# Moving 195 of 8832 row gathers from GpSimd to SyncE, row by row

## The chip, the cores and the metric

The kernel runs on one core of a Trainium2 chip. The metric is device time in microseconds, from the start of the program to its end. Five engines work beside each other, each with its own queue of instructions: TensorE (PE), VectorE (DVE), ScalarE (ACT), GpSimd (POOL) and SyncE (SP). Transfers between the chip's memory and the on-chip buffers are issued by SyncE or GpSimd and carried out by 16 DMA engines that both share.

## The reference

A recommendation model scores 16384 users. Each has 69 ids of a table of 100001 embeddings of 96 numbers, and one label id. For every (user, id) pair the embedding `u` and the label's embedding `q` go through a small attention network, which gives one weight; the weighted embeddings are summed in 10 groups and go through three dense layers.

```
u   = emb[batch_user]                          # (16384, 69, 96)
ql  = emb[batch_label[:, 0]];  q = broadcast(ql)
z   = concat([q, u, q - u, q * u])             # (..., 384)
h   = dice(z @ W1 + b1, a1)                    # 64
att = (h @ W2 + b2) @ W3 + b3                  # one number
pre = where(batch_user < ITEM_NUM, u * att, 0)
pooled = einsum('gf,bfe->bge', window, pre)    # 10 groups
x   = concat([pooled, ql])
x   = dice(bn(x @ Wf1 + bf1));  x = dice(bn(x @ Wf2 + bf2))
out = x @ Wf3 + bf3
```

`dice(x)` is `(alpha (1 - p) + p) x` with `p` the sigmoid of `x` scaled. What matters here is the first line: 16384 x 69 rows of 384 bytes, scattered over the table, must be fetched.

## The kernel before

The users are cut into 32 blocks of 512 (`NBLK`, `BLK`). A block has 69 chunks (`NCH`) of 512 (user, id) pairs: 64 main chunks, in each of which 8 users stand with 64 ids (`NMAIN`), and 5 tail chunks, each with one further id for all 512 users (`NTAIL`). Two chunks make a pair of chunks, the step of the main loop; there are 32 x 69 / 2 = 1104 pairs (`NPAIR`). "Pair" means this below.

A chunk's rows come as four tiles of 128 rows, one row per partition. Each tile is one indirect DMA, issued by GpSimd in `gather`:

```python
gather(rows, u[:, 4 * j + t, :], ids[n][:, 4 * k + t : 4 * k + t + 1])
nc.tensor.transpose(ptr[:, t * P : (t + 1) * P], u[:, 4 * j + t, :], ident)
```

So a pair has 8 gathers, into a buffer `u` of a pool of 14 (`upool`), and the kernel has 1104 x 8 = 8832. Each block has 4 more gathers for its labels (`head_gather`), 128 in all. In `fetch`, TensorE transposes each of the four tiles into one PSUM buffer `ptr`; VectorE multiplies that with the label's embedding (`quT`) and ScalarE copies it (`uT`). `hidden` makes the first layer of the attention network two pairs later, `attend_rows` and `spread` the weights, and `pool(i)`, 7 pairs later (`POOL_LAG`), multiplies the same rows `u` with these weights: it is the last reader of a tile of rows. The dense layers of a finished block (`top1`, `top2`, `top3`) are spread over later pairs.

The order of all this is written out by hand: `at(step, work)` puts each piece of work into a plan by pair number, and the plan is run in order under a manual schedule. Each engine's queue keeps that order; only the waits between engines are put in by the framework.

SyncE has 13 DMAs: the first block's ids, two packs of weights (`wn`, `wf`), 8 loads of ids for 4 blocks each (`load_ids`, planned 20 pairs ahead of their first use), and two stores of the result.

Of the kernel before, what the change touches and what calls it, by code (L numbers as in the profile page):

```python
# [1 line left out]

# [7 lines left out]

F32 = mybir.dt.float32
I32 = mybir.dt.int32
AF = mybir.ActivationFunctionType
ALU = mybir.AluOpType
PSUM = bass.MemoryType.PSUM

P = 128
B, F, E, G = 16384, 69, 96, 10  # L40
ITEM_NUM = 100000
# [5 lines left out]
NBLK = B // BLK  # L47
FM = 64
NTAIL = F - FM
NS = BLK // FM  # L50
NMAIN = BLK // NS
NCH = NMAIN + NTAIL
# [12 lines left out]
EARLY = 20  # L65

CLOSE = 8


class Pack:  # L70
# [44 lines left out]
def rec_kernel(  # L115
# [3 lines left out]
    idx: bass.AP,  # L119
    emb: bass.AP,  # L120
    rows: bass.AP,
    near: bass.AP,
    far: bass.AP,
    out: bass.AP,
):
    nc = tc.nc

    const = ctx.enter_context(tc.tile_pool(name="const", bufs=1))
    ipool = ctx.enter_context(tc.tile_pool(name="ipool", bufs=2))
# [7 lines left out]
    def by_field(ap):  # L137

        return ap.rearrange("e (s o) -> e s o", o=1).to_broadcast([ap.shape[0], NS, FM])

    ids = {0: const.tile([P, NCOL], I32, name="ids0")}
    nc.sync.dma_start(out=ids[0], in_=idx0)

    def load_ids(n):

        t = ipool.tile([P, NIDS, NCOL], I32, tag="ids", name=f"ids{n}")
        nc.sync.dma_start(out=t.rearrange("p b n -> p (b n)"), in_=idx[(n - 1) // NIDS])
        for k in range(NIDS):
            ids[n + k] = t[:, k, :]


    wn = const.tile([P, NEAR.width], F32, name="wn")
    nc.sync.dma_start(out=wn, in_=near)
# [3 lines left out]
    ident = const.tile([P, P], F32, name="ident")  # L157
# [26 lines left out]
    for i in range(2):  # L184
        t = const.tile([E + 1, BLK], F32, name=f"qT{i}")
# [70 lines left out]
    def gather(table, dst, index):  # L256
        nc.gpsimd.indirect_dma_start(  # L257
            out=dst,
            out_offset=None,
            in_=table,  # L260
            in_offset=bass.IndirectOffsetOnAxis(ap=index, axis=0),
        )

    def chunk(c):

        n, k = divmod(c, NCH)
        if n == NBLK - 1 and k >= EARLY:
            k = NMAIN + k - EARLY if k < EARLY + NTAIL else k - NTAIL
        return n, k

    def head_gather(n):

# [28 lines left out]
    def fetch(i, between=None):  # L301

        u = upool.tile([P, 8, E], F32, tag="u", name=f"u{i}")
        uT = []
        quT = tpool.tile([E, 2, 512], F32, tag="quT", name=f"quT{i}")
        for j in range(2):
            if j == 1 and between:
                between()
            n, k = chunk(2 * i + j)
            ptr = ps_tr.tile([E, 512], F32, tag="tr", name=f"ptr{i}_{j}")  # L310
            for t in range(4):
                gather(rows, u[:, 4 * j + t, :], ids[n][:, 4 * k + t : 4 * k + t + 1])
                nc.tensor.transpose(ptr[:, t * P : (t + 1) * P], u[:, 4 * j + t, :], ident)  # L313
            q = qTs[n % 2][0:E]
            if k < NMAIN:
                nc.vector.tensor_tensor(  # L316
                    quT[:, j, :].rearrange("e (s f) -> e s f", f=FM),
                    ptr.rearrange("e (s f) -> e s f", f=FM),
                    by_field(q[:, k * NS : (k + 1) * NS]),
                    ALU.mult,  # L320
                )
            else:
                nc.vector.tensor_tensor(quT[:, j, :], ptr, q[:, 0:BLK], ALU.mult)
            uT.append(room(k))
            nc.scalar.copy(uT[j][0:E], ptr)  # L325
        return u, uT, quT

    def hidden(i, uT, quT):

        ph = ps_h.tile([P, 512], F32, tag="h", name=f"ph{i}")  # L330
        places = [chunk(2 * i + j) for j in range(2)]
# [25 lines left out]

    def attend_tail(i, j, y, uT):

        n, k = chunk(2 * i + j)  # L360
# [26 lines left out]
    def pool(i):  # L387

        u, rw = us.pop(i), rws.pop(i)
        todo = [(j, *chunk(2 * i + j)) for j in range(2)]  # L390
        todo = [(j, n, k) for j, n, k in todo if k < NMAIN]
        if not todo:
            return
        pa = ps_acc.tile([E, 2, NS, G], F32, tag="acc", name=f"acc{i}")
        for j, n, k in todo:
            for t in range(4):
                nc.tensor.matmul(  # L397
                    pa[:, j, 2 * t : 2 * t + 2, :].rearrange("e n g -> e (n g)"),
                    u[:, 4 * j + t, :],
                    rw[:, t, j, :],  # L400
                    start=True,
                    stop=True,
                )
        if len(todo) == 2:
# [98 lines left out]
    def hidden_of(k):  # L503
        return lambda: ys.__setitem__(k, hidden(k, *hs[k]))

    def tails_of(k):
        def work():
            uT = hs.pop(k)[0]
            for j in range(2):
                if chunk(2 * k + j)[1] >= NMAIN:  # L510
                    attend_tail(k, j, ys[k], uT)

        return work

    def fetch_of(k, between=()):
        def work():
            for j in range(2):
                n = chunk(2 * k + j)[0]
# [11 lines left out]
    def at(step, *work):  # L530
        plan.setdefault(step, []).extend(work)

    c = NPAIR - CLOSE
    for i in range(c):
# [6 lines left out]
        if i >= 2:  # L541
            at(i, hidden_of(i - 2))
        if i < c - CLOSE:
            if i >= POOL_LAG:
# [16 lines left out]
    for n in range(NBLK):  # L561
        first, end = n * NCH // 2, ((n + 1) * NCH - 1) // 2
        if n > 0:
            if n % NIDS == 1:
                at(first - 20, lambda n=n: load_ids(n))
            at(first - 14, lambda n=n: qs.__setitem__(n, head_gather(n)))
            at(first - 11, lambda n=n: head_turn(n, qs.pop(n)))
            at(first - 9, lambda n=n: head_rows(n))
        if n < NBLK - 2:
            for s, work in enumerate(top_steps(n, slice(0, BLK))):  # L570
                at(end + POOL_LAG + 4 + s, work)
        elif n == NBLK - 2:
            for s, work in enumerate(top_steps(n, slice(0, BLK))):
                at(end + POOL_LAG + s // 2, work)
    for f in range(NTAIL):
        at(2 + 2 * f, lambda f=f: tail_weights(f))

# [6 lines left out]
    d = NPAIR  # L584
# [75 lines left out]
```

## Time and profile before

| | |
|---|---|
| timed runs | 13386.58, 13436.96, 13456.45 us; median 13436.96 us |
| profiled execution, span of its instructions | 11239.3 us (no other time of that execution is given) |
| GpSimd busy | 8465.4 us, 75% of the span |
| TensorE busy | 9082.8 us, 81% |
| ScalarE, VectorE busy | 3188.3 us, 3014.3 us |
| gathers of rows | 8832, mean 945 ns each |
| bytes read | 446.61 MB, 40 GB/s over the span |
| mean granted TensorE clock | 0.727 |

The profile is that of one execution. All times in it are measured from the span's start. The timed median is 2197.7 us longer than the profiled span. An engine's busy time leaves out instructions that only issue DMAs, set registers or wait, so SyncE has no busy time at all; its DMA issues stand as "SPq" in the timeline. A group's row gives the line, engine, operation, tiles, count and busy time with the mean of one, and behind the bar the idle time in front of these instructions and what ended most of it ("issue": nothing that the profile shows).

### The profile page before, as it was taken

The page shows a single profiled execution, that of the slowest core. Times are in us where ns is not written, and L with a number is a line of the kernel's source. Part 1 is how long each engine was busy: PE and PEld are TensorE (multiplying, and loading weights), DVE is VectorE, ACT ScalarE, POOL GpSimd, SP SyncE. Part 2 cuts the span into 40 slices and gives each one's busy share as a digit, 9 for nine tenths or more (in the row PEclk, how much of TensorE's full clock was granted, in tenths as well). Part 3 has the DMA queues.
Part 4 walks back from the last instruction along what each step waited for, and adds up shares of the span by engine and source line. Part 5 has one row for each costly group of instructions (what it writes and reads, how often), then busy time and mean ns, then how long its engine had stood idle before and what let it go on. Part 6 is the DMA issues. An engine that isn't in the chain of part 4 may idle for free.

```text
span 11239.3 us, 108444 instructions
## 1 busy us (share of the span) xinstructions
PE 9082.8 (81%) x41797; PEld 4395.1 (39%) x41797; DVE 3014.3 (27%) x5325; ACT 3188.3 (28%) x4969; POOL 8465.4 (75%) x8966
## 2 busy tenths in 40 slices
PE   7888888888878787877888778777787887888888
PEld 3333433333433333333333333333343333433335
DVE  3222222222222222222222222222222222222222
ACT  2222222222222222222222222222222222222223
POOL 7777777777777777777777777777777777777776
PEclk6767777677776777777777777777777767777767
DMA  2111111111111111111111111111111111111111
GB/s 49 40 40 40 40 40 42 40 40 40 40 42 40 40 40 40 42 40 40 40 40 42 40 40 40 40 42 40 40 40 40 42 40 40 40 40 40 40 40 35
DMA packets 288946, 454.19 MB, mean 40 GB/s; under 512 B 143538, under 2 KB 143922, under 8 KB 288306
## 3 DMA queue, kind: packets, MB, share of 16 engines
q0 software_dynamic: 286720, 440.98, 18.7%
q8 instruction: 335, 5.49, 0.2%
q1 hardware_dynamic: 1714, 6.28, 0.2%
q14 instruction: 177, 1.45, 0.0%
HBM read 446.61 MB, written 0.07 MB: 40 GB/s over the span
## 4 chain that ended last, share of the span: by engine, by line
POOL 51%; issue 23%; PE 15%; DMA 11%; ACT 0%; DVE 0%; POOLq 0%
POOL u L257 50%; DMA u<-in_rows,ids 11%; PE p L438 4%; PE acc L397 3%; PE ph L342 2%; PE ph L338 2%; PE ptr L313 2%; POOL q L257 1%; PE prow L353 1%; PE ph L335 1%; PE ph L340 0%; PE pc L290 0%; PE pa L362 0%; PE patt L370 0%; PE p L449 0%
## 5 line engine op out<-in xcount | busy, mean ns | idle before, releaser
L257 POOL DMA_INDIRECT u<-in_rows,ids x8832 | 8343.6, 945 | 2690.9 <-issue 2510.2
L313 PE MATMUL ptr<-ident,u 128*96 128x128 f32 x8832 | 2092.4, 336 | 2080.2 <-DMA u<-in_rows,ids 2066.4
L325 ACT COPY uT<-ptr 96x512 f32<-96x512 f32 x2208 | 1285.2, 582 | 4422.4 <-DVE quT L316 4069.1
L313 PEld LDWEIGHTS ptr<-ident,u 128*96 128x96 f32 x8832 | 1184.6, 150 | 2904.1 <-DMA u<-in_rows,ids 2460.6
L397 PEld LDWEIGHTS acc<-rw,u 128*96 128x96 f32 x16384 | 1746.1, 190 | 1206.4 <-issue 1059.7
L346 DVE TENSOR_TENSOR y<-ph,y 128x512 f32<-128x512 f32 x1104 | 763.5, 692 | 4885.1 <-ACT y L345 4703.4
L316 DVE TENSOR_TENSOR quT<-ptr,qT 96x512 f32<-96x512 f32 x2048 | 1375.9, 677 | 2183.2 <-PE ptr L313 2180.0
L397 PE MATMUL acc<-rw,u 128*96 128x20 f32 x16384 | 1852.9, 260 | 23.1 <-DVE rw L375 18.0
L338 PE MATMUL ph<-uT,A 128*64 128x512 f32 x4096 | 1688.2, 902 | 1.0 <-ACT uT L325 1.0
L342 PE MATMUL ph<-quT,wn 96*64 96x512 f32 x4416 | 1628.4, 809 | 0.0
L344 ACT ACTIVATE y<-ph 128x512 f32<-128x512 f32 x1104 | 659.4, 597 | 2971.7 <-PE ph L342 2962.3
L345 ACT ACTIVATE y<-y,wn,na1c 128x512 f32<-128x512 f32 x1104 | 898.1, 814 | 37.3
L342 PEld LDWEIGHTS ph<-quT,wn 96*64 96x64 f32 x4416 | 447.5, 191 | 1070.4 <-issue 1069.8
L438 PE MATMUL p<-pooled,wf 96*100 96x512 f32 (+1 forms) x1400 | 706.2, 654 | 0.0
L338 PEld LDWEIGHTS ph<-uT,A 128*64 128x64 f32 x4096 | 269.0, 179 | 616.0 <-issue 609.8
L406 DVE COPY pooled<-acc 96x160 f32<-96x160 f32 x1008 | 419.9, 417 | 129.4 <-PE acc L397 129.4
L353 PE MATMUL prow<-y,v 128*32 128x512 f32 x2208 | 452.4, 894 | 0.3 <-DVE y L346 0.3
L438 PE MATMUL p<-pre,V 96*100 96x512 f32 (+1 forms) x700 | 398.9, 717 | 2.7 <-DVE x L421 2.3
L438 PEld LDWEIGHTS p<-pooled,wf 96*100 96x100 f32 x1400 | 265.6, 202 | 341.2 <-issue 341.2
L375 DVE SCALAR_TENSOR_TENSOR rw<-patt,bb,wn 128x320 f32<-128x320 f32 x554 | 277.8, 543 | 221.2 <-PE patt L370 220.3
L355 ACT COPY row<-prow 128x512 f32<-128x512 f32 (+1 forms) x277 | 161.8, 584 | 314.5 <-PE prow L353 314.2
L370 PE MATMUL patt<-ident,row 128*128 128x128 f32 x1108 | 231.2, 347 | 15.9 <-DVE pre L363 15.2
(66 smaller groups left out, 2227.6 us busy)
## 6 DMA issues: line engine op xcount, KB each, us to landing
u<-in_rows,ids POOLq DMA_INDIRECT x8832, 2.5
ids<-in_idx SPq DMA_DIRECT2D x8, 560.0 KB, 3.7
q<-in_emb,ids POOLq DMA_INDIRECT x128, 2.5
wf<-in_far SPq DMA_DIRECT2D x1, 1209.0 KB, 7.8
wn<-in_near SPq DMA_DIRECT2D x1, 236.0 KB, 2.7
ids<-in_idx SPq DMA_DIRECT2D x1, 140.0 KB, 2.2
out<-r SPq DMA_DIRECT2D x1, 63.5 KB
out<-r SPq DMA_DIRECT2D x1, 0.5 KB
```

Source lines behind the costliest of these rows:

```text
L257: nc.gpsimd.indirect_dma_start(out=dst, out_offset=None, in_=table, in_offset=bass.IndirectOffsetOnAxis(ap=index, axis=0),)
L313: nc.tensor.transpose(ptr[:, t * P : (t + 1) * P], u[:, 4 * j + t, :], ident)
L316: nc.vector.tensor_tensor(quT[:, j, :].rearrange("e (s f) -> e s f", f=FM), ptr.rearrange("e (s f) -> e s f", f=FM), by_field(q[:, k * NS ...
L325: nc.scalar.copy(uT[j][0:E], ptr)
L338: nc.tensor.matmul(p, As[n % 2][:, k // 4, :], uT[j], start=True, stop=False)
L342: nc.tensor.matmul(p, Wp, quT[:, j, :], start=False, stop=True)
L344: nc.scalar.activation(y, ph, AF.Sigmoid, scale=S_DICE)
L345: nc.scalar.activation(y, y, AF.Identity, bias=a1c, scale=na1c)
L346: nc.vector.tensor_mul(y, ph, y)
L353: nc.tensor.matmul(pr[32 * k : 32 * (k + 1), :], v2, ys[b + k], start=True, stop=True)
L397: nc.tensor.matmul(pa[:, j, 2 * t : 2 * t + 2, :].rearrange("e n g -> e (n g)"), u[:, 4 * j + t, :], rw[:, t, j, :], start=True, stop=True,)
L438: nc.tensor.matmul(p1, w[:, h * DH : (h + 1) * DH], x, start=(k == 0), stop=(k == KTOP - 1))
```

## The change

195 tiles of rows are no longer gathered by GpSimd. Tile `s` is the last (`SLOT` 3) of the four tiles of the second chunk of pair `int(5.5 * s) + 6`, so one tile is taken in each 5.5 pairs, from pair 6 to pair 1073. SyncE fetches its 128 rows with 128 plain DMAs of one row of 384 bytes each. Their addresses are byte offsets into the table: a new input `single` holds the 195 x 128 row numbers, which VectorE multiplies by 3 and shifts left by 7 (x 384) once at the start; SyncE then loads them 32 at a time into registers, in four loads per tile. The rows go into a ring of 7 buffers of its own. Every row adds 16 to one of 14 semaphores, which the tiles use in turn, and TensorE waits once per tile, until the count of all 128 rows is reached. Before SyncE writes into a ring buffer again, it waits for the last reader of the tile that was in it. Tile `s` is planned 6 pairs ahead of its use. The loads of ids are planned 50 pairs ahead of use, not 20. (`chunk` is renamed `chunk_of` and moved out of the kernel function.)

```diff
+SINGLES = [(int(5.5 * s) + 6) * 2 + 1 for s in range(195)]
+SLOT = 3
+NRING = 7
+NSEM = 14
+IDS_AT_ONCE = 32
...
+    row_bytes = rows.bitcast(U8).rearrange("(o n) k -> o (n k)", o=1)
...
+    offsets = const.tile([P, NSB, P], I32, name="offsets")
+    nc.sync.dma_start(out=offsets.rearrange("p b r -> p (b r)"), in_=single)
+    nc.vector.tensor_scalar(offsets, offsets, 3, None, ALU.mult)
+    nc.vector.tensor_scalar(offsets, offsets, 7, None, ALU.logical_shift_left)
...
+    def single_tile(s):
+        b, k = s % NRING, s % NSEM
+        at = offsets[s % P : s % P + 1, s // P]
+        new = []
+        for g in range(0, P, IDS_AT_ONCE):
+            _, values = nc.values_load_multi_w_load_instructions(
+                at[:, g : g + IDS_AT_ONCE],
+                engines=[mybir.EngineType.SP],
...
+            for r, v in enumerate(values, g):
+                d = nc.sync.dma_start(
+                    out=ring[r : r + 1, b], in_=row_bytes[:, bass.ds(v, ROW_BYTES)]
+                ).then_inc(sems[k], 16)
...
+        given[k] += 16 * P
+        singles[SINGLES[s]] = b, sems[k], given[k]
...
             for t in range(4):
-                gather(rows, u[:, 4 * j + t, :], ids[n][:, 4 * k + t : 4 * k + t + 1])
-                nc.tensor.transpose(ptr[:, t * P : (t + 1) * P], u[:, 4 * j + t, :], ident)
+                c = 2 * i + j
+                if t == SLOT and c in singles:
+                    nc.tensor.wait_ge(singles[c][1], singles[c][2])
+                else:
+                    gather(rows, u[:, 4 * j + t, :], ids[n][:, 4 * k + t : 4 * k + t + 1])
+                ins = nc.tensor.transpose(ptr[:, t * P : (t + 1) * P], rows_of_slot(u, c, j, t), ident)
...
-                    u[:, 4 * j + t, :],
+                    rows_of_slot(u, 2 * i + j, j, t),
...
-                at(first - 20, lambda n=n: load_ids(n))
+                at(max(0, first - 50), lambda n=n: load_ids(n))
...
+    for s, m in enumerate(SINGLES):
+        at(m // 2 - 6, lambda s=s: single_tile(s))
```

More of the change, by code (lines that the diff above doesn't have):

```diff
@@ L34 @@
 I32 = mybir.dt.int32
+U8 = mybir.dt.uint8
 AF = mybir.ActivationFunctionType
@@ L67, with chunk_of @@
 CLOSE = 8
+SINGLES = [(int(5.5 * s) + 6) * 2 + 1 for s in range(195)]
+SLOT = 3
+ROW_BYTES = 4 * E
+NSB = (len(SINGLES) + P - 1) // P
+NRING = 7
+NSEM = 14
+IDS_AT_ONCE = 32
+def chunk_of(c):
+    n, k = divmod(c, NCH)
+    if n == NBLK - 1 and k >= EARLY:
+        k = NMAIN + k - EARLY if k < EARLY + NTAIL else k - NTAIL
+    return n, k
 class Pack:
@@ L121, in rec_kernel @@
     rows: bass.AP,
+    single: bass.AP,
     near: bass.AP,
@@ L124, in rec_kernel @@
     out: bass.AP,
+    ring: bass.AP,
 ):
     nc = tc.nc
+    row_bytes = rows.bitcast(U8).rearrange("(o n) k -> o (n k)", o=1)
     const = ctx.enter_context(tc.tile_pool(name="const", bufs=1))
@@ L262, in gather, with rows_of_slot, reads_single @@
         )
[L264 to L269, printed above, removed]
+    sems = [tc.alloc_semaphore(f"singles{k}") for k in range(NSEM)]
+    singles, given = {}, [0] * NSEM
+    def single_tile(s):
[6 more added lines that the diff above has]
+                engines=[mybir.EngineType.SP],
+                min_val=0,
+                max_val=ITEM_NUM * ROW_BYTES,
+                skip_runtime_bounds_check_because="offsets of rows of the table",
+            )
+            for r, v in enumerate(values, g):
+                d = nc.sync.dma_start(
+                    out=ring[r : r + 1, b], in_=row_bytes[:, bass.ds(v, ROW_BYTES)]
+                ).then_inc(sems[k], 16)
+                tc.no_tile_sem_insts.add(d.ins.name)
+                tc.declare_no_dep(d.ins, group=f"ring{b}", reason="a buffer's readers have waited for its rows")
+                new.append(d.ins)
+        for ins in new:
+            tc.add_to_no_dep_group(f"ring{b}", ins)
+        given[k] += 16 * P
+        singles[SINGLES[s]] = b, sems[k], given[k]
+    def rows_of_slot(u, c, j, t):
+        if t == SLOT and c in singles:
+            return ring[:, singles[c][0]].bitcast(F32)
+        return u[:, 4 * j + t, :]
+    def reads_single(c, t, ins):
+        if t == SLOT and c in singles:
+            tc.declare_no_dep(ins.ins, group=f"ring{singles[c][0]}", reason="waited for by semaphore")
     def head_gather(n):
@@ L308, in fetch @@
                 between()
-            n, k = chunk(2 * i + j)
+            n, k = chunk_of(2 * i + j)
             ptr = ps_tr.tile([E, 512], F32, tag="tr", name=f"ptr{i}_{j}")
             for t in range(4):
-                gather(rows, u[:, 4 * j + t, :], ids[n][:, 4 * k + t : 4 * k + t + 1])
-                nc.tensor.transpose(ptr[:, t * P : (t + 1) * P], u[:, 4 * j + t, :], ident)
+                c = 2 * i + j
+                if t == SLOT and c in singles:
+                    nc.tensor.wait_ge(singles[c][1], singles[c][2])
+                else:
+                    gather(rows, u[:, 4 * j + t, :], ids[n][:, 4 * k + t : 4 * k + t + 1])
+                ins = nc.tensor.transpose(ptr[:, t * P : (t + 1) * P], rows_of_slot(u, c, j, t), ident)
+                reads_single(c, t, ins)
             q = qTs[n % 2][0:E]
@@ L330, in hidden @@
         ph = ps_h.tile([P, 512], F32, tag="h", name=f"ph{i}")
-        places = [chunk(2 * i + j) for j in range(2)]
+        places = [chunk_of(2 * i + j) for j in range(2)]
         sums = [ph[j * H1 : (j + 1) * H1, :] for j in range(2)]
@@ L358, in attend_tail @@
     def attend_tail(i, j, y, uT):
-        n, k = chunk(2 * i + j)
+        n, k = chunk_of(2 * i + j)
         pa = ps_x.tile([E, 512], F32, tag="x", name=f"pa{i}_{j}")
@@ L389, in pool @@
         u, rw = us.pop(i), rws.pop(i)
-        todo = [(j, *chunk(2 * i + j)) for j in range(2)]
+        todo = [(j, *chunk_of(2 * i + j)) for j in range(2)]
         todo = [(j, n, k) for j, n, k in todo if k < NMAIN]
@@ L396, in pool @@
             for t in range(4):
-                nc.tensor.matmul(
+                ins = nc.tensor.matmul(
                     pa[:, j, 2 * t : 2 * t + 2, :].rearrange("e n g -> e (n g)"),
-                    u[:, 4 * j + t, :],
+                    rows_of_slot(u, 2 * i + j, j, t),
                     rw[:, t, j, :],
@@ L403, in pool @@
                 )
+                reads_single(2 * i + j, t, ins)
         if len(todo) == 2:
@@ L509, in work @@
             for j in range(2):
-                if chunk(2 * k + j)[1] >= NMAIN:
+                if chunk_of(2 * k + j)[1] >= NMAIN:
                     attend_tail(k, j, ys[k], uT)
@@ L517, in work @@
             for j in range(2):
-                n = chunk(2 * k + j)[0]
+                n = chunk_of(2 * k + j)[0]
                 if n not in pooled:
@@ L620, in side_by_side @@
         return a.reshape(n, -1, a.shape[1]).transpose(1, 0, 2).reshape(-1, n * a.shape[1])
+    singles = np.zeros((P, NSB, P), np.int32)
+    for s, m in enumerate(SINGLES):
+        n, k = chunk_of(m)
+        singles[s % P, s // P] = ids[n][:, 4 * k + SLOT]
     arrays = {
@@ L626 @@
         "rows": np.concatenate([x["emb"][:ITEM_NUM], np.zeros((1, E), np.float32)], axis=0),
+        "single": singles.reshape(P, -1),
         "near": NEAR.fill(
@@ L655 @@
     out = nc.dram_tensor("out_0", (B, 1), F32, kind="ExternalOutput").ap()
+    ring = nc.alloc_sbuf_tensor("ring", [P, NRING, ROW_BYTES], U8).ap()
     with tile.TileContext(nc) as tc:
-        rec_kernel(tc, *args, out)
+        rec_kernel(tc, *args, out, ring)
     r = run_bass_kernel_spmd(nc, [arrays], core_ids=[0])
```

## The prediction

> **What bounds the kernel now.** I read four views, in this order: the page's busy times, its groups with the chain that ended last, the timeline of GpSimd, and SyncE's rows.
>
> The busy times name no winner: TensorE is busy 81% of the span and GpSimd 75%. The groups and the chain decide.
>
> ```profile
> span 11239.3 us, 108444 instructions
> PE 9082.8 (81%) x41797; PEld 4395.1 (39%) x41797; DVE 3014.3 (27%) x5325; ACT 3188.3 (28%) x4969; POOL 8465.4 (75%) x8966
> POOL 51%; issue 23%; PE 15%; DMA 11%; ACT 0%; DVE 0%; POOLq 0%
> L257 POOL DMA_INDIRECT u<-in_rows,ids x8832 | 8343.6, 945 | 2690.9 <-issue 2510.2
> L313 PE MATMUL ptr<-ident,u 128*96 128x128 f32 x8832 | 2092.4, 336 | 2080.2 <-DMA u<-in_rows,ids 2066.4
> ```
>
> GpSimd's gathers and the gap in front of each ("issue", in which it waits for nothing) make 74% of the chain. TensorE, busier on paper, sat 2066 us in front of its transposes until a gather had landed. The timeline of GpSimd shows how regular this is:
>
> ```profile
> 8000.09 0.94 POOL L257 DMA_INDIRECT u<-in_rows,ids  x1 [0.30 <-issue]
> 8001.34 0.94 POOL L257 DMA_INDIRECT u<-in_rows,ids  x1 [0.30 <-issue]
> 8002.58 0.94 POOL L257 DMA_INDIRECT u<-in_rows,ids  x1 [0.30 <-DMA u<-in_rows,ids]
> ...
> 8015.07 0.94 POOL L257 DMA_INDIRECT u<-in_rows,ids  x1 [0.30 <-issue]
> ```
>
> From 8000.09 to 8015.07 there are 12 steps: 14.98 / 12 = 1.248 us each. There are 8832 gathers of rows and 128 of labels, and 8960 x 1.248 = 11182 us, all but 57 us of the span. So GpSimd never stops, and the kernel takes as long as it has gathers. The gap named "DMA u" is as long as the others, so no landing holds GpSimd.
>
> SyncE, which gets the new work, has almost none. Its timeline and the rows of its own line:
>
> ```profile
> 0.75 0.41 SPq L142 DMA_DIRECT2D ids<-in_idx  x1
> 1.21 0.42 SPq L153 DMA_DIRECT2D wn<-in_near  x1
> 11226.30 0.32 SPq L466 DMA_DIRECT2D out<-r  x1
> 11237.14 0.25 SPq L474 DMA_DIRECT2D out<-r  x1
> L147 SPq DMA_DIRECT2D ids<-in_idx x8: 327/328/432, 2.1 to 8756.5; - x8
> ```
>
> The price that matters is the last store (L474): one row of 512 bytes, 0.25 us to issue. A load of 128 rows costs 0.33 us once running (L147, median 328 ns). Between the first two issues 0.05 us lie free (1.21 - 0.75 - 0.41).
>
> [...]
>
> **The change, part by part.** The program's order shows that it does what it says: GpSimd has 8765 gathers instead of 8960, SyncE 24960 row DMAs (195 x 128) and 780 register loads of 32 values.
>
> *Removed:* 195 gathers x 1.248 = 243.4 us of the engine that sets the end. New GpSimd time 8765 x 1.248 = 10939, plus the 57 us around it: span 10996.
>
> *Scale.* The page gives a span and no further time for the profiled execution. The median of the timed runs, 13436.96, is 1.1955 times that span. A gather there would take 1.4920 us; [...] I take it that everything, SyncE included, is stretched alike: 10996 x 1.1955 = 13146 us. If the 2197.7 us were instead a fixed stretch outside the span, it would be 13194. Taken: 13150.
>
> *Added on SyncE, which must hide.* Tile s is read in pair int(5.5 s) + 6: one tile per 5.5 pairs. In that time GpSimd issues 5.5 x 8 - 1 = 43 gathers of rows and 4 x 5.5 / 34.5 = 0.64 of labels: 43.64 x 1.248 = 54.5 us. SyncE's time for a tile has to stay below this. A row issue is at least 0.25 + 0.05 = 0.30 us (L474); at most, I say, 0.33 + 0.05 = 0.38 (L147), since it has one row but takes its address from a register with a bound. No row of before shows the register form; I take 0.33. The 128 rows: 38.4, 42.2 or 48.6 us. A register load isn't in the trace either. [...] The sum: [...] **50.2 taken, 4.3 below the limit**[...].
>
> *Around it.* The ring has 7 buffers. A buffer is free after its pooling, 7 pairs after its transposes, so SyncE can be about five tiles ahead; single delays don't show, only its rate. The load of ids (L147) now stands among the row DMAs in SyncE's queue, but 30 pairs earlier than before, some 300 us; its waits are for gathers long past. The row DMAs' data: the store at L474 is two packets[...], and gathers have 2.5 us to landing that GpSimd doesn't wait for. TensorE gets 181 more wait instructions; the nearest row, GpSimd's own semaphore waits, is 17 ns, so 3 us, inside its 2156 us of idle time. Behind such a wait stand all later transposes, and through the 14 buffers of u GpSimd itself, about 7 pairs later. VectorE gets two small operations at the start, where the first gathers hide them. I cost these at nothing; if their cover went, SyncE's rate would have been the reason.
>
> **Rivals.**
>
> *Slower: SyncE becomes the bound.* Above 54.5 us per tile TensorE waits for the ring, and GpSimd stops behind it. The end is then 5 us + 195 tiles + the 31 pairs left after pair 1073 (31 x 8 x 1.248 = 310 us). Equality with before is at (11239 - 315) / 195 = 56.0 us per tile, so the turn is sharp: from 54.8 to 56.0 the whole gain is lost. [...] For it: [...] 8% of slack is little. Against it: [...] the cheapest row observed is of the very shape that is issued.
>
> *No change: TensorE is the bound in the timed runs.* Then the gathers are hidden anyway and 13437 stays. Against it: TensorE needs 9083 of 10996 us, 17% to spare, and the stretch of 1.1955 would have to be its alone. A SyncE tile at just 56 us also ends here.
>
> *Half a gain: gathers slow down beside the row packets.* The gathers' 286720 packets took 18.7% of 16 engines' span: 0.187 x 16 x 11239 / 286720 = 0.117 us each. Even at that price a row's two packets make 128 x 2 x 0.117 = 30 us in 54.5 of one engine in 16, and less if they are spread. GpSimd waits for no landing, which speaks against it. If each gather still lost 1% of its pace, 110 us of the span, the time would be 13280.
>
> *The change doing something else* is excluded by the instruction counts.
>
> **How the numbers follow.** GpSimd stays the bound and the gain arrives, whole or in most part: 0.68 (13060 to 13300, likeliest 13150). TensorE bound, or SyncE at 55.7 to 56.3 us: 0.05. SyncE the bound beyond that: 0.27, spread from 13500 to 17700[...]. A difference of 0.5%, 67 us, is about what a measurement of this kernel can tell from no change; the three runs span 70 us. So faster 0.68, same 0.05, slower 0.27. The likeliest case and the equal one hold 0.73; to leave out no more than 0.2 the range goes on into the slower case as far as a tile of 58.9 us: (195 x 58.9 + 315) x 1.1955 = 14107. Range 13060 to 14100.
>
> **What would show it.** Right: 8637 gathers in GpSimd's group for u, still at 1.248 us from start to start without holes; a span near 10996; SyncE's waits mostly for TensorE's pooling, which frees a ring buffer; next to no time of TensorE on the ring. Wrong: TensorE's waits led by DMAs into the ring, holes in GpSimd every 5.5 pairs, and SyncE with no wait at all; then its register loads or row issues, summed per tile, exceed 54.5 us, and the timeline tells which of the two prices failed. A gather pace above 1.26 us would speak for contention instead.

## The result, and the profile after

The change made the kernel slower: 15650.24 us median (15624.16 to 15673.66, 4 runs) against 13446.70 us (13386.58 to 13486.93, 4 runs), a ratio of 1.1648, 95% interval 1.1609 to 1.1687. One thing has to be known to read the numbers that follow: the kernel before takes about 11230 us on some chips and 13320 to 13450 us on others (medians), each of them steadily. The profile that the prediction read is of the first kind (span 11239.3 us), the times that it was to forecast are of the second, and so is the profile after.

From the page of the changed kernel: the span, the busy times, the chain that ended last by engine and by line, and the groups of the gathers and of the transposes that read the ring.

```profile
span 15671.9 us, 159138 instructions
PE 8577.3 (55%) x41797; PEld 4549.6 (29%) x41797; DVE 2985.9 (19%) x5327; ACT 3140.5 (20%) x4969; POOL 8270.2 (53%) x8771
SPq 62%; issue 35%; PE 1%; another core or an unknown queue 0%; ACT 0%; DVE 0%; DMA 0%; DVEq 0%
SPq L286 53%; SPq L278 9%; PE p L479 0%; PE ph L378 0%; PE acc L437 0%; PE ptr L352 0%; PE ph L382 0%; DMA ring<-in_rows 0%; PE patt L410 0%; ACT uT L365 0%; ACT y L385 0%; PE prow L393 0%; DVE quT L356 0%; ACT y L384 0%
L262 POOL DMA_INDIRECT u<-in_rows,ids x8637 | 8148.3, 943 | 7261.6 <-PE ptr L352 2487.6
L352 PE MATMUL ptr<-ident,ring 128*96 128x128 f32 x195 | 82.2, 422 | 4071.9 <-DMA ring<-in_rows 3861.9
```

No engine is busy for even 56% of the span. The chain is SyncE's queue: its row DMAs (L286) and register loads (L278) are 62%, and 35% is "issue", time between instructions in which nothing shown was waited for. The 195 transposes that read the ring had TensorE idle for 4072 us in front of them, and GpSimd's largest idle time ends on a transpose. The view of waits has the same two links with their counts, and GpSimd's timeline shows what they look like:

```profile
PE ptr L352 <- DMA ring<-in_rows: 3861.9, 180, 48.3
POOL u L262 <- PE ptr L352: 2487.6, 236, 47.6
```

```profile
8039.57 0.95 POOL L262 DMA_INDIRECT u<-in_rows,ids  x1 [0.30 <-issue]
8040.82 0.94 POOL L262 DMA_INDIRECT u<-in_rows,ids  x1 [0.30 <-issue]
8071.33 0.94 POOL L262 DMA_INDIRECT u<-in_rows,ids  x1 [29.56 <-PE ptr L352]
8072.57 0.94 POOL L262 DMA_INDIRECT u<-in_rows,ids  x1 [0.31 <-issue]
```

While it runs, a gather still starts every 1.25 us. Then there is a hole of 30 us: SyncE's tile is late, TensorE waits for it (35.85 us before its transpose of the ring at 8063.50), and GpSimd waits for TensorE (29.56 us). These are the signs that the prediction had named for its slower rival, SyncE as the bound. The rows of SyncE's own lines (each with its count, its durations in ns as least, median and greatest, and its first and last start) tell more:

```profile
L278 SPq TENSOR_LOAD <-offsets x780: 5/2124/2391, 4.0 to 15268.1; - x195
L286 SPq MOVE ring<-in_rows x24960: 1/29/1422, 6.2 to 15290.6; - x200
L286 SPq DMA_DIRECT2D ring<-in_rows x24960: 1/228/1423, 6.3 to 15292.0; - x200
```

By its medians a row is a move to a register and an issue, 0.322 us from start to start in quiet stretches, and a load is 2.1 us: 128 x 0.322 + 4 x 2.12 = 49.7 us per tile, within 1% of the 50.2 us predicted. But the mean from the first load of one tile to that of the next is 78.3 us. The greatest durations show where the rest is: a move to a register, 29 ns by the median, took up to 1.42 us. The trace has these long instructions in steps of about 0.70 us, and in the neighbourhood of gathers: with none started in the last 5.5 us a row takes 0.33 us on average, with four or more 0.85 us. The fetching of instructions is too rare to be the reason: its two queues carried 336 + 571 = 907 packets in all, and 5197 of SyncE's moves and issues took 0.6 to 0.8 us.

### The profile page after: what moved, and what is told of

Read it like the earlier page. It is cut to its first block, busy times and chain, and to the rows that moved or that the text cites. A ratio compares the mean times of both kernels' runs of the same rounds, so it can differ in the third digit from the quotient of the medians.

```text
span 15671.9 us, 159138 instructions
## 1 busy us (share of the span) xinstructions
PE 8577.3 (55%) x41797; PEld 4549.6 (29%) x41797; DVE 2985.9 (19%) x5327; ACT 3140.5 (20%) x4969; POOL 8270.2 (53%) x8771
## 4 chain that ended last, share of the span: by engine, by line
SPq 62%; issue 35%; PE 1%; another core or an unknown queue 0%; ACT 0%; DVE 0%; DMA 0%; DVEq 0%
SPq L286 53%; SPq L278 9%; PE p L479 0%; PE ph L378 0%; PE acc L437 0%; PE ptr L352 0%; PE ph L382 0%; DMA ring<-in_rows 0%; PE patt L410 0%; ACT uT L365 0%; ACT y L385 0%; PE prow L393 0%; DVE quT L356 0%; ACT y L384 0%
## 5 line engine op out<-in xcount | busy, mean ns | idle before, releaser
L262 POOL DMA_INDIRECT u<-in_rows,ids x8637 | 8148.3, 943 | 7261.6 <-PE ptr L352 2487.6
L437 PE MATMUL acc<-rw,u 128*96 128x20 f32 x16026 | 1932.4, 265 | 1503.2 <-issue 921.4
L437 PEld LDWEIGHTS acc<-rw,u 128*96 128x96 f32 x16026 | 1824.6, 198 | 2517.8 <-issue 1621.3
L352 PE MATMUL ptr<-ident,ring 128*96 128x128 f32 x195 | 82.2, 422 | 4071.9 <-DMA ring<-in_rows 3861.9
L356 DVE TENSOR_TENSOR quT<-ptr,qT 96x512 f32<-96x512 f32 x2048 | 1329.0, 674 | 3702.0 <-PE ptr L352 2628.8
L352 PE MATMUL ptr<-ident,u 128*96 128x128 f32 x8637 | 1558.1, 333 | 800.4 <-issue 616.6
L382 PE MATMUL ph<-quT,wn 96*64 96x512 f32 x4416 | 1533.3, 706 | 96.3 <-issue 87.2
L378 PE MATMUL ph<-uT,A 128*64 128x512 f32 x4096 | 1522.2, 786 | 60.3 <-issue 55.5
L479 PE MATMUL p<-pooled,wf 96*100 96x512 f32 (+1 forms) x1400 | 665.2, 617 | 13.4 <-issue 12.0
L393 PE MATMUL prow<-y,v 128*32 128x512 f32 x2208 | 550.3, 800 | 93.3 <-issue 46.9
```

The costliest lines, as they stand in the source:

```text
L262: nc.gpsimd.indirect_dma_start(out=dst, out_offset=None, in_=table, in_offset=bass.IndirectOffsetOnAxis(ap=index, axis=0),)
L352: ins = nc.tensor.transpose(ptr[:, t * P : (t + 1) * P], rows_of_slot(u, c, j, t), ident)
L356: nc.vector.tensor_tensor(quT[:, j, :].rearrange("e (s f) -> e s f", f=FM), ptr.rearrange("e (s f) -> e s f", f=FM), by_field(q[:, k * NS ...
L437: ins = nc.tensor.matmul(pa[:, j, 2 * t : 2 * t + 2, :].rearrange("e n g -> e (n g)"), rows_of_slot(u, 2 * i + j, j, t), rw[:, t, j, :], s ...
L479: nc.tensor.matmul(p1, w[:, h * DH : (h + 1) * DH], x, start=(k == 0), stop=(k == KTOP - 1))
```

## Experiments

**Does SyncE slow down beside gathers?** (`e1_unread`) Theory A at this point: gathers slow SyncE's rows. The kernel keeps all 8832 gathers of before; SyncE makes 60 tiles that nobody needs, of five kinds, 50 beside the gathers and 10 after the last one.

```diff
+        kind = s // 10 if s < 50 else (s - 50) // 2
...
+                if kind == 0:     # a row by register address, as in the change
+                elif kind == 1:   # four semaphore increments and no DMA
+                elif kind == 2:   # the row as 16 pieces of 24 bytes
+                elif kind == 3:   # from on-chip memory, fixed address
+                else:             # a row from a fixed address
```

> GpSimd gathers all 8832 tiles as before; SyncE fetches extra rows that no result uses (one matmul that writes nothing of use reads each ring buffer, 80 pairs later). 50 tiles run beside the gathers in five stretches of ten: (0) row DMAs as in the change, (1) four semaphore increments of SyncE per row and no DMA at all, (2) 16 pieces of 24 bytes per DMA, one for each of 16 partitions, (3) rows out of SBUF instead of HBM, no register address, split in 16 pieces, (4) rows from HBM at fixed addresses. Two more tiles of each kind follow when the gathers are over. Theory A, SyncE's rows are slowed by the gathers: kind 0 takes about 0.95 us per row beside gathers and 0.32 us after them. Rival B, a row simply costs more than one DMA issue, gathers or not (78 us per tile): the same mean pitch in both places. If the slowing is one of DMAs, the increments of kind 1 keep their pace in both places; if SyncE's sequencer as a whole is held up, they slow too. [...]if it is HBM, only kind 3 is free of it; if it is the register address, kind 4 is. Gathers keep 1.25 us from start to start.

This run fell on a chip where the kernel before takes 11229.6 us; it took 11779.84 us itself, since its last tiles come after the last gather. The rows of the lines for kind 0 and kind 1, ns least, median, greatest:

```profile
L291 SPq MOVE ring<-in_rows x1536: 29/29/38, 5.8 to 11338.8; - x192
L291 SPq DMA_DIRECT2D ring<-in_rows x1536: 224/225/444, 5.8 to 11338.9; - x192
L294 SPq EVENT_SEMAPHORE  x6144: 3/17/71, 1351.3 to 11402.4; - x199
```

No move takes above 38 ns and no increment above 71. The median step is the same beside the gathers and after them, within 0.004 us: 0.322 us for a register row (0.319 beside), 0.29 for a fixed one, 0.46 in 16 pieces, 0.63 from on-chip memory, 0.059 for an increment. Gathers stay at 1.249 us. So here gathers don't slow SyncE. Both prices that the prediction needed hold: a row took 0.322 us here (0.33 taken), and a load of 32 registers 2.12 us by its median in the changed kernel (L278; 2.0 taken, the author's estimate, since no trace of before shows a load).

**Fewer tiles.** One tile per 11 and per 16 pairs, on the same chip; nothing else changes.

```diff
-SINGLES = [(int(5.5 * s) + 6) * 2 + 1 for s in range(195)]
+SINGLES = [(int(11 * s) + 6) * 2 + 1 for s in range(98)]
```

> 98 tiles instead of 195, one per 11 pairs. Rival B (a tile costs SyncE 78 us whatever runs beside it): the 110 us that GpSimd needs for 11 pairs cover it, 98 x 1.25 = 122 us of gathers are gained, ratio to before 0.99. Theory A (0.95 us per row while gathers run): a tile needs about 130 us beside gathers, SyncE stays the bound, 98 x 117 us and 350 us around them, a span near 11800 us, which is above the profiled span of before.

> 67 tiles, one per 16 pairs (159 us of GpSimd's time). Both theories let SyncE keep up here (130 or 78 us per tile): TensorE next to never waits for the ring, GpSimd runs without holes, and 67 x 1.25 = 84 us are gained on the span of before, ratio 0.993. If it is slower all the same, a single row tile costs TensorE or GpSimd something that is not SyncE's rate.

98 tiles: 11107.86 us against 11229.6, ratio 0.9891 (0.9875 to 0.9908), 122 us less; 98 x 1.249 = 122. 67 tiles: 11149.83 us, 0.9929 (0.9912 to 0.9945), 80 us less; 67 x 1.249 = 84. On such a chip each gather that goes to SyncE is saved whole, within the intervals. In the waits of SyncE's queue in the first of them, the DMAs wait for TensorE's last use of a ring buffer, and so SyncE is ahead:

```profile
SPq L286 <- PE ptr L352: 5004.9, 80, 120.0
```

**The change again, one tile per 8 pairs, fixed addresses, and the kernel before with a profile**, on one chip, which was of the other kind. `e6_fixed` is the change without its loads and register addresses.

```diff
-SINGLES = [(int(5.5 * s) + 6) * 2 + 1 for s in range(195)]
+SINGLES = [(int(8 * s) + 6) * 2 + 1 for s in range(134)]      # e5_sparse8 alone
...
-            _, values = nc.values_load_multi_w_load_instructions(   # e6_fixed alone
-                    out=ring[r : r + 1, b], in_=row_bytes[:, bass.ds(v, ROW_BYTES)]
+                    out=ring[r : r + 1, b], in_=row_bytes[:, r * ROW_BYTES : (r + 1) * ROW_BYTES]
```

> The changed kernel itself, a second time. Theory A (SyncE's row is slow because of the kernel: gathers, or its own packets) expects about 15600 us again, 195 tiles x 78.3 us plus 315 us of ends, wherever it runs. Theory B (the rows were slow because of the conditions of that run; undisturbed, a row takes the 0.322 us that the unread rows and the sparse tiles took) expects a tile of 128 x 0.322 + 4 x 2.15 = 49.8 us under the 54.5 us that one tile per 5.5 pairs allows, so GpSimd stays the bound and the time is 11230 - 195 x 1.249 = 10986 us, ratio 0.978, if the kernel before takes 11230 us beside it; if the kernel before takes about 13440 us beside it, B expects 15600 us again.

> 134 tiles, one per 8 pairs (79 us of gathers). Theory B expects 11230 - 134 x 1.249 = 11063 us where the kernel before takes 11230 us. Theory A expects SyncE's tile at its 78.3 us to just fit: 11063 to 11300 us. Where the kernel before takes about 13440 us, either is read from the pitch of the rows: 0.322 us or 0.61 us.

> As the changed kernel with its 195 tiles, but SyncE fetches the first 128 rows of the table for every tile, at addresses written in the instructions: it leaves out the register loads and the moves to registers, and with them the right rows. A tile costs SyncE 128 x 0.292 = 37.4 us by the unread rows of the earlier run. Theory B expects 10986 us beside 11230 us for the kernel before, the same as the changed kernel beside it. If register loads and register addresses are what is held up (theory C), this one gains 243 us even where the changed kernel loses; if every SyncE instruction is (theory A or B), it loses there too, only less: its row pitch would go up by the same factor of about 1.9.

> The kernel before, profiled where the others run. Theory B expects a gather pitch of 1.249 us and 11230 us where the changed kernel is at 10986 us; and if this run falls at about 13440 us, the pitch of the gathers and the waits for TensorE in the profile show what makes that time: 1.5 us per gather if GpSimd is slower itself, 1.249 us with holes that end on TensorE if TensorE is.

Beside 13440.53 us for the kernel before: the change 15630.56 us, ratio 1.1627 (1.1599 to 1.1656); 134 tiles 13527.82 us, 1.0060 (1.0039 to 1.0081); fixed addresses 13438.05 us, 1.0002 (0.9994 to 1.0011). Rows that took 0.322 us on the other chip are slow again here, so theory B, that the conditions of the run decide, is borne out. The 134 tiles took SyncE 94 us each on average, longer than the 78.3 us of the change and than the 80 us of gathers in 8 pairs: what a tile costs isn't one number. Theory C, that only register loads and register addresses are held up, falls: with fixed addresses SyncE's DMAs still come late, by about 0.70 or 1.40 us, and the gain is gone.

```profile
L278 SPq DMA_DIRECT2D ring<-in_rows x24960: 2/252/1426, 3.1 to 12721.8; - x200
```

The kernel before, profiled here, shows what the condition is. Its page (span, busy times, chain, the gathers and one ScalarE group):

```profile
span 13443.0 us, 108444 instructions
PE 9013.5 (67%) x41797; PEld 4530.8 (34%) x41797; DVE 3027.8 (23%) x5325; ACT 3142.4 (23%) x4969; POOL 8455.3 (63%) x8966
PE 53%; another core or an unknown queue 21%; issue 15%; DVE 5%; ACT 4%; POOL 2%; DMA 0%; DVEq 0%; POOLq 0%; ACTq 0%
L257 POOL DMA_INDIRECT u<-in_rows,ids x8832 | 8333.2, 944 | 4849.7 <-issue 2375.5
L345 ACT ACTIVATE y<-y,wn,na1c 128x512 f32<-128x512 f32 x1104 | 898.0, 813 | 36.6
```

Against the page that the prediction read, nothing is slower by itself: a gather is 944 ns (945 there), the activation 813 ns (814 there), the median step of the gathers 1.249 us. The activation's row there:

```profile
L345 ACT ACTIVATE y<-y,wn,na1c 128x512 f32<-128x512 f32 x1104 | 898.1, 814 | 37.3
```

Only the idle times grew, that in front of GpSimd's gathers by 2159 us, and the chain went from GpSimd (51%) to TensorE (53%). The timeline shows TensorE's weight loads (PEld) beside the gathers:

```profile
6038.52 0.45 PEld L313 LDWEIGHTS ptr<-ident,u 128*96 128x96 f32 x4
...
6039.50 0.13 PEld L313 LDWEIGHTS ptr<-ident,u 128*96 128x96 f32 x1 [0.53 <-issue]
6040.19 0.94 POOL L257 DMA_INDIRECT u<-in_rows,ids  x1 [0.30 <-issue]
...
6040.90 0.17 PEld L313 LDWEIGHTS ptr<-ident,u 128*96 128x96 f32 x2 [1.28 <-issue]
...
6041.44 0.94 POOL L257 DMA_INDIRECT u<-in_rows,ids  x1 [0.30 <-issue]
...
6042.34 0.16 PEld L313 LDWEIGHTS ptr<-ident,u 128*96 128x96 f32 x1 [1.27 <-issue]
6042.68 0.94 POOL L257 DMA_INDIRECT u<-in_rows,ids  x1 [0.30 <-issue]
...
6043.74 0.24 PEld L438 LDWEIGHTS p<-pre,V 96*100 96x100 f32 x1 [1.25 <-issue]
```

At 6038.52 four loads follow each other in 0.45 us. Then, with nothing to wait for ("issue"), the next come in steps of 1.40, 1.44 and 1.40 us, twice 0.70, while GpSimd goes on every 1.25 us. I call this the hold-up: TensorE's and SyncE's instructions are let through late, in steps of about 0.70 us, and GpSimd's are not. VectorE's don't show it either: in this trace and in that of the change each of the 1104 products `y` starts within 34 ns of the last thing that it needed, ScalarE's activation or VectorE's own instruction before.

**What the gain is worth without its price, what instructions alone cost, and half the gathers.** `e8_none` fetches only the first 7 ring tiles. `e9_seminc` issues one row and 255 semaphore increments per tile after the first 7. `e10_half` is the kernel before with every second gather left out; TensorE reads the neighbouring tile instead, so its work stays.

```diff
+        if s >= NRING:                                   # e8_none
+            singles[SINGLES[s]] = b, sems[b], 16 * P
+            return
...
+            for r in range(255):                         # e9_seminc, after one row
+                nc.sync.sem_inc(ticks[r % 10], 1)
...
+                if t % 2 == 0:                           # e10_half
                     gather(rows, u[:, 4 * j + t, :], ids[n][:, 4 * k + t : 4 * k + t + 1])
```

> As the changed kernel, but only the first 7 ring tiles are fetched; the other 188 tiles are read from what the ring holds, so SyncE does nothing for them and the rows are wrong: the gain of 195 fewer gathers without any of its price. Theory D (where the kernel before takes 13440 us it is bound by TensorE, whose instructions are held up, and not by GpSimd) expects no gain there: 13400 to 13440 us. Theory E (SyncE's instructions are what eats the gain) expects the full 195 x 1.249 = 244 us or, stretched, 290 us less: 13150 to 13200 us. If the kernel before takes 11230 us beside it, both expect 10986 us.

> As the changed kernel, but from the 8th tile on SyncE issues one row from a fixed address and 255 semaphore increments per tile in place of 128 rows with loads (the rows are wrong): as many SyncE instructions, hardly a DMA. Undisturbed a tile takes 255 x 0.059 = 15 us. If every SyncE instruction is held up while gathers are issued (theory F), increments are spaced by about 0.7 us in places and a tile takes 50 us or more; if only DMA issues and register work are (theory G), they keep 0.059 us. Time: where the kernel before takes 13440 us, not above 13500 us; where it takes 11230 us, 10986 us.

> The kernel before with every second gather left out (4416 for u instead of 8832; each slot without one is read from its neighbour, so the sums are wrong). All of TensorE's work stays. Undisturbed TensorE is then the bound at about its 9083 us of busy time, 9100 to 9500 us. Theory F (instructions of the other engines are held up while GpSimd issues gathers) expects, where the kernel before takes 13440 us, about half of the hold-up left: TensorE's 4350 us of excess over 9083 becomes 2200, so 11000 to 11500 us. Theory H (that chip holds all instructions up regardless of gathers) expects about 13300 us still.

On a chip where the kernel before takes 13349.86 us: 195 gathers less and no SyncE work give 13182.71 us, ratio 0.9877 (0.9853 to 0.9900). Theory D (no gain) and theory E (a gain of 244 us or more) both miss; the time lies in the 13150 to 13200 us that E had named only because the kernel before is faster on this chip. 167 us, 0.86 us per gather (0.68 to 1.0 by the interval), is what there was to win here. With the increments it is 13372.25 us in one run, nothing won: some 48000 increments, with 188 DMAs among them, cost 190 us and with that the gain. Their line, and their mean spacing while gathers run, by how many gathers the latest one has before it in an unbroken run (from the starts in the trace; undisturbed 0.059 us):

```profile
L284 SPq EVENT_SEMAPHORE  x47940: 1/17/1403, 651.3 to 12727.2; - x200
```

```
gathers before it in the run     0-1    2-3    4-7    8-11   12-15   16 and more
mean spacing of increments, us   0.15   0.29   0.40   0.69   0.96    1.28
```

So theory F (every SyncE instruction is held up during runs of gathers) holds on this chip and G (only DMAs and registers) falls: the longer GpSimd has gathered without a pause, the longer the hold-up. Half the gathers took it away: 7847.33 us, with TensorE busy 89% of the span.

```profile
span 7845.6 us, 104028 instructions
PE 6994.7 (89%) x41797; PEld 3757.2 (48%) x41797; DVE 2940.8 (37%) x5325; ACT 3145.3 (40%) x4969; POOL 4287.7 (55%) x4550
```

That is far below the 11000 to 11500 us that F had expected and the 9100 us that I took for TensorE's own minimum: its mean granted clock was 0.912 here and 0.723 to 0.727 in the kernel before beside it. Within the bursts of pooling (L397 in the kernel before), the kernel before, as `e7_before` shows it, had 216 of 15350 steps from one weight load to the next above 0.45 us (6 on the first kind of chip); here there are 9.

**The change twice more, and gathers further apart.** The paced kernels are the kernel before with a memset on GpSimd after each gather for `u`, of 64, 160 or 288 values.

```diff
                 gather(rows, u[:, 4 * j + t, :], ids[n][:, 4 * k + t : 4 * k + t + 1])
+                nc.gpsimd.memset(idle, 0.0)
```

> The changed kernel once more, on whatever chip it falls. Where the kernel before takes about 11230 us beside it (no instruction held up), a SyncE tile takes 49.8 us under the 54.5 us allowed and the time is 10986 us, ratio 0.978. Where the kernel before takes 13350 to 13440 us, 15600 us again, ratio 1.163 to 1.17.

> The kernel before with a small memset (64 values in each partition) on GpSimd after each of the 8832 gathers for u, guessed at 0.1 to 0.25 us, so that gathers start every 1.35 to 1.5 us. Undisturbed GpSimd is the bound and the time rises to 11900 to 13300 us. Where the kernel before takes about 13400 us because long runs of gathers hold up the other engines more and more (0.06 us per SyncE instruction at the first gather of a run, 1.4 us at the 17th), theory F expects the wider spacing to take the hold away: the same 11900 to 13300 us as the undisturbed one, less than 13400. If the hold-up depends only on how many gathers are made, it stays, and the time is 13400 us or more.

> The kernel before with a memset of 160 values per partition on GpSimd after each gather for u: by the last run (64 values: 166 ns, starts every 1.282 us)[...], 0.235 us and a gather every 1.35 us, 12100 us where nothing is held up. If the spacing decides the hold-up (theory F), the hold is smaller than at 1.282 us and the time is between 12200 and 13000 us, below the kernel before; if the number of gathers decides, about 13250 us again, as at 1.249 and 1.282 us.

> As the run before with 288 values: about 0.325 us, a gather every 1.44 us, 12900 us where nothing is held up. Theory F expects hardly any hold left and 12900 to 13000 us; the other theory 13250 us or more.

> The changed kernel on one more chip. Beside a kernel before of about 11230 us: 10986 us, SyncE rows every 0.322 us, GpSimd without holes. Beside one of 13330 to 13440 us: 15400 to 15650 us again.

The change: 15428.82 us beside 13332.97, ratio 1.1582 (1.1558 to 1.1605), and on the chip of `e8_none` again 15415.96 us. It lost on three of the second kind of chip. The paced kernels, one run each (GpSimd's idle time: what its starts lie apart beyond the step; the last column again in the bursts of pooling):

```
step of gathers   memset    time     before beside it   GpSimd's idle time   steps above 0.45 us
1.249 us          none      13444.8  13440.5            2159 us              216
1.282 us          0.166 us  13262.8  13333.0            1672 us              380
1.365 us          0.246 us  13168.4  13322.7             854 us              560
1.468 us          0.352 us  13197.4  13322.7              26 us                6
```

The first memset mostly fitted into the gap behind a gather, so `e12_paced` told little. At 1.365 us F had asked for 12200 to 13000 us and got 13168: the hold-up is still there, with more late steps than without a memset, though GpSimd stops less. At 1.468 us it is gone. The time misses the 12900 to 13000 us expected since the step is 1.468 us and not 1.44: 8832 x 1.468 + 128 x 1.249 + 57 = 13182 us, and measured 13197.

What fits all four rows is a limit on the rate: the kernel before makes one gather per 1.47 to 1.50 us on average on these chips (13167 / 8960 = 1.47 to 13443 / 8960 = 1.50). When GpSimd issues them faster, the others are held up until TensorE is late and GpSimd has to stop for it; when it issues them no faster, nobody is held up, and the time is nearly the same. That is a reading of four traces and not shown: no step between 1.365 and 1.468 us was met on such a chip, and with SyncE's work beside them the gathers come further apart, 1.53 us in `e6_fixed` (13438 / 8765) and 1.79 us in the change. At 1.468 us the kernel is the prediction's one again, in chain and waits:

```profile
POOL 73%; issue 10%; PE 10%; DMA 7%; POOLq 0%; DVE 0%; ACT 0%
PE ptr L315 <- DMA u<-in_rows,ids: 3336.0, 3300, 2.1
```

**The change with paced gathers.** A smaller ring (4 and 5 tiles) makes room for the memset's buffer.

```diff
-NRING = 7
+NRING = 5                                    # 4 with 288 values
...
                     gather(rows, u[:, 4 * j + t, :], ids[n][:, 4 * k + t : 4 * k + t + 1])
+                    nc.gpsimd.memset(idle, 0.0)
```

> The kernel before with a memset of 224 values on GpSimd after each gather for u: by 246 ns at 160 and 352 ns at 288 values a memset of 0.30 us and a gather every 1.416 us, 8832 x 1.416 + 128 x 1.25 + 57 = 12723 us where nothing is held up. If the hold-up is a threshold that lies below 1.416 us, 12700 to 12800 us beside about 13330 us; if above, 13100 us with idle time on GpSimd.

> The changed kernel with the memset of 288 values after each of its 8637 gathers for u, and a ring of 4 tiles instead of 7 to make room. The paced kernel before took 13197 us. Theory F (only the hold-up made SyncE late) expects SyncE's rows at 0.322 us, a tile of 49.8 us in 5.5 pairs of 62 us, and 13197 - 195 x 1.467 = 12911 us. If SyncE's own 50000 instructions bring the hold-up back, rows over 0.4 us, holes in GpSimd and more than 13200 us; if they are slow for a cause of their own, 15400 us again.

> The changed kernel with the memset of 224 values and a ring of 5 tiles: 195 x 1.416 = 276 us less than the paced kernel before at 224 values, about 12450 us, if that one is free of the hold-up and SyncE does not bring it back; otherwise SyncE is held up and the time is above that of the paced kernel before, by theory F up to 195 x 70 us + 350 us = 14000 us.

These three fell on a chip of the first kind, 11229.71 us for the kernel before, where pacing can only cost. So they don't tell whether SyncE's own instructions bring the hold-up back at 1.468 us on the second kind; that stays open. What they show is the change's own working at its full 195 tiles: paced kernel before 12731.03 us, paced change 12464.15 us with 224 values. 267 us less where 195 x 1.414 = 276 was due; with 288 values 12916.30 us, 5 us from the expectation. SyncE's rows and its wait for the ring in the first of these:

```profile
L287 SPq MOVE ring<-in_rows x24960: 29/29/29, 6.2 to 11889.6; - x200
L287 SPq DMA_DIRECT2D ring<-in_rows x24960: 227/228/567, 6.3 to 11889.6; - x200
SPq L287 <- PE ptr L354: 1933.4, 163, 21.9
```

All 24960 moves took 29 ns: no hold-up. A tile takes SyncE 51.0 us (the 5th percentile over the tiles, those with hardly a wait), and it has 163 waits for a free buffer.

## Why the prediction was wrong

- **What bounds the kernel.** Right for the profile that it read: on that kind of chip GpSimd sets the end, and 98 gathers less were 122 us less. Wrong for the times that it was to forecast. There TensorE, held up, led the chain (53%), and 195 gathers less without any work on SyncE were worth 167 us on the chip where that was run, not 291.
- **The scale: the step that failed.** "I take it that everything, SyncE included, is stretched alike." This was the author's estimate; the two numbers behind its 1.1955, a timed median and the span of one profile, show no longer duration. Nothing was stretched: the median step of the gathers stayed 1.249 us where the prediction had 1.492, and an activation took 813 ns, 814 in the profile that it read. Instead TensorE and SyncE let instructions through late while GpSimd gathered. A stretch common to all leaves SyncE's margin as it was, 60.0 us for a tile under a limit of 65.2 (50.2 and 54.5 x 1.1955); the hold-up took it away.
- **SyncE's tile: the term that was mis-sized.** The two guessed prices were right where nothing is held up: 0.322 us for a row (0.33 taken), 2.1 us for a load of 32 registers from on-chip memory (2.0 taken, so 8 for the four loads of a tile), a tile of 49.7 to 51.0 us (50.2 taken). But beside the gathers of these chips the tile took 78.3 us, and the prediction allowed for no such cause. The prediction's own formula, without the scale, accounts for the time with it: 5 + 195 x 78.3 + 31 x 8 x 1.50 = 15646 us, measured 15650. That is no second proof, since the 78.3 us are from the same run.
- **The slower rival** had the right bound and the right waits, and its ground that 8% of slack is little held. Its other ground, a dear register load, was the author's estimate, which no trace showed, and it was wrong: by their median the four loads of a tile took 4 x 2.12 = 8.5 of its 78.3 us. Neither of the two prices failed; the hold-up came on top of both.
- **The rival "TensorE is the bound in the timed runs"** was turned down since "the stretch of 1.1955 would have to be its alone". The delay was TensorE's and SyncE's, and not GpSimd's. With cheaper SyncE work (`e6_fixed`) that rival's outcome came true: 1.0002.
- **Gathers slowed beside the row packets**: no. Their median step was 1.249 to 1.252 us in every trace without a memset.
- **The ring, the loads of ids, TensorE's extra waits** cost next to nothing where nothing is held up: 267 of 276 us arrived in the paced pair.

What is shown is that on these chips close gathers bring the hold-up (half of them, or gathers 1.468 us apart, take it away), and that late SyncE work is what loses the 2200 us (without it, in `e8_none`, they aren't lost). What stays open: why two of the five chips on record for these runs hold nothing up and three do, and whether it is the chip or the moment, since one chip alone was met twice; what the instructions are held up by; and whether the trace's own recording has a part in it, since no run here is without. The unpaced change was never met on a chip of the first kind. By the sparse kernels it should take 11230 - 195 x 1.249 = 10986 us there, an estimate. Apart from the kernel before, no version was met on both kinds of chip, so none is known to be the best on both. On the first kind the best was the one with 98 tiles (11107.86 us, 1.1% under the kernel before); on the second, of those that fetch all rows, the kernel before paced at 1.365 us (13168.41 us, 1.2% under, a single run).

## What to carry to other kernels

When the timed median and the span of the profile differ by a fifth, suspect that the profile is of another condition than the times: first profile the kernel before again beside timed runs, and compare the mean durations, the steps and the idle times in the two traces, before any cost is scaled. Work that is moved to an idle queue is priced by its own durations, but also by whether that queue runs freely while the bounding engine works: a margin of 8% for a stream of 50000 small instructions was none here. And where GpSimd issues gathers without a pause, don't count a saved gather at its full time until a run without any replacement has shown what it is worth: 1.249 us on one kind of chip here, 0.86 us on the other.

## What the runs showed of the hardware that I had not expected

- On three of five chips the kernel before took 13320 to 13450 us and not 11230. In the traces from there, the instructions of TensorE (weight loads, `e7_before`) and SyncE (moves of up to 1.42 us in the change, increments of up to 1.40 us in `e9_seminc`) come late in steps of about 0.70 us beside runs of indirect DMAs 1.25 us apart, and VectorE's products `y` don't (34 ns at most behind what they need). The hold-up grows with the run (0.15 us per increment at its start, 1.28 us after 16 gathers, `e9_seminc`) and is gone in pauses (0.33 us per row of the change with no gather in the last 5.5 us). Gathers and their data aren't touched: the first packet follows a gather's start by 1.65 us and the last by 2.16 us (medians) on both kinds of chip.
- On those chips the kernel before made one gather per 1.47 to 1.50 us on average whether GpSimd issued one each 1.249, 1.282, 1.365 or 1.468 us.
- A memset of 64 values per partition (0.166 us) between two gathers moved their step only from 1.249 to 1.282 us.
- With half the gathers TensorE's mean granted clock rose from about 0.725 to 0.912, and the kernel took 7847 us.
